# A transformer block in fp32: a new order for its beginning and its end, and a modulation moved between two heads

## The chip, the core and the metric

The kernel runs on one core of a Trainium2 chip. The metric is the device time of one execution in microseconds (us). A core has TensorE (PE, matrix products, with weight loads beside them), VectorE (DVE), ScalarE (ACT), GpSimd (POOL) and SyncE (SP, which here only issues DMA transfers). Each engine works through its own list of instructions in order and waits on semaphores for the others. PE writes into PSUM, eight banks of 128 partitions x 512 fp32 values; DVE and ACT read from there.

## What is computed

One block with adaptive layer norm for two sequences (B = 2) of 1024 rows of 256 values: 16 heads of 128, and a gated feed-forward layer of 704 hidden values with quantised weights.

```python
mod = (silu(c) @ wmod).reshape(B, 6, 1, -1)        # c is 2 x 256
sa, ca, ga, sb, cb, gb = the six parts of mod
ga = (2 * (ga >= 0) - 1) * maximum(abs(ga), 0.25)  # gb likewise
h = layernorm(x) * (1 + ca) + sa
x = x + ga * attention(h)       # rotary q, k; causal softmax; biases on q, k, v, out
h = layernorm(x) * (1 + cb) + sb
x = x + gb * (W_down(silu(W_gate h) * (W_up h)))   # W = (wq - 128) * scale per row
```

## The kernel before

All products are fp32, and PE runs each as two passes, so the profile counts two matmuls for one in the code. A layer norm is split: `ln_stats` and `ln_scale` (DVE) and `ln_sqrt` (ACT) make normalised rows `xn`, `ln_turn` transposes a block of four row tiles on PE, 128 x 128 at a time, and writes `hT` with scale and shift, one half by DVE and (with `split`) one by ACT. Later layer norms inside the loop over heads go another way, by DVE transposes and DMAs (`ln_move`, `ln_send`, `ln_shift`). `modulation(which, ...)` makes shift and scale columns as products of wmod with SiLU(c); `gates` makes the two gate rows and spreads them over the partitions through DRAM.

The order of work is written out by hand (`tc.manual_schedule`), so program order is the order on each engine. It has three stages.

- The beginning (lines 646 to 693): constants, loads, the first layer norm, q, k and v of the first head in two blocks of 512 rows. On SP the loads are issued in the order x tiles 0 and 1, half of the first wmod block, x tiles 2 and 3, the other half, wq, wk, half of the rotary tables, wv, x tiles 4 to 7, the other half of the tables, wga, the second wmod block, the weights of later heads. ACT issues c (as a column over 128 partitions) and the biases. `warm_up` products of ones keep PE occupied while the loads are under way: three at the start and one after each of the four groups of the first modulation.
- The loop over 32 heads (lines 695 to 735), index n, with eight steps i each: scores of row block i, the masked maximum on DVE, the exponential on ACT, DVE transposes of the probabilities in blocks of 32, 32 DMAs per head issued by SP to complete the transposition (pT), products with the values, the output projection; and beside them the projections of the next head. `extras` places further work; the modulation of the second layer norm and its `shift_scale` stand there at n = 0, i = 6.
- The end (lines 737 to 770): the last hidden chunks (`hidden`, six per block of 512 rows, the sixth of 64 + 64 rows), the last layer norm blocks, the down products (`down`) and the stores.

PSUM is divided into pools: ps_a (two banks), ps_o and ps_y (one each), ps_sc (two pairs of banks, for scores of up to 1024 columns). A tile taken from a pool waits until the previous holder of its bank has been read. `bank` deals out y, o, a, a in turn at the end. In SBUF, `rot` has two buffers (tag r1), `xnp` four; outputs of the first block of the first sequence use `rot`, the others `xnp`.

In `down`, the sixth chunk has only 64 rows; these rows lie in the upper half of the partitions for odd row tiles and in the lower half for even ones, so that two such passes run at the same time. They come after the five full chunks, for two row tiles at a time (first block of the first sequence, last block of the second) or for all four.

Of the kernel before, what the change touches and what calls it, by code (L numbers as in the profile page):

```python
# [37 lines left out]
def adaln_block(ctx: ExitStack, tc: tile.TileContext, a, cos_d, sin_d, out):  # L38
# [21 lines left out]
    wmod = fpool.tile([P, 2, KC, 2 * D], F32, tag="f", name="wmod")  # L60
# [5 lines left out]
    nc.scalar.dma_start(sc, a["L0_c"])  # L66
    for n in range(KC):
        load_x(0, 2 * n, 2, nc.sync)
        half = slice(n * D, (n + 1) * D)
        nc.sync.dma_start(wmod[:, 0, :, half], a["L0_wmod"][0, :, :, half])  # L70
    nc.scalar.dma_start(cols, a["biases"])

# [11 lines left out]
    for n in range(3):  # L84
        warm_up(4)
# [26 lines left out]
    def modulation(which, pool, tag):  # L112

        pm = pool.tile([P, 512], F32, tag=tag, name=f"pm{which}")
        for n in range(2):
            for f in range(KC):
                at = (n * KC + f) * B
                for k in range(KC):
                    nc.tensor.matmul(
                        pm[:, at : at + B],  # L120
                        wmod[:, which // 2, k, n * D + f * P : n * D + (f + 1) * P],
                        sc[:, :, k],
                        start=(k == 0),
                        stop=(k == KC - 1),
                    )
                if not which:
                    warm_up(1)
        pms[which] = pm
# [3 lines left out]
    def shift_scale(which):  # L132
        pm = pms[which]
        for n in range(2):
            nc.vector.tensor_scalar(
                modT[:, which + n].rearrange("p f b -> p (f b)"),
                pm[:, n * KC * B : (n + 1) * KC * B],
                float(n),
                None,
                ALU.add,  # L140
            )
# [3 lines left out]

    def gates():

        pg = ps_y.tile([P, 512], F32, tag="y", name="pg")
        for k in range(KC):
            nc.tensor.matmul(pg[:B], sc[:, :, k], wga[:, k, :], start=(k == 0), stop=(k == KC - 1))  # L150
# [55 lines left out]
    def ln_turn(b, name, blk, which, dest, split=False):  # L206
        for f in range(KC):
            pt = ps_a.tile([P, 512], F32, tag="a", name=f"ptx_{name}{b}_{blk}_{f}")
            for j in range(4):
                nc.tensor.transpose(  # L210
                    pt[:, ts(j, P)], xns[b, name, 4 * blk + j][:, ts(f, P)], ident
                )
            shift, scale = (modT[:, which + n, f, b : b + 1] for n in range(2))
            if split and f:
                nc.scalar.activation(dest[:, f, :], pt, AF.Identity, bias=shift, scale=scale)
            else:
                nc.vector.tensor_scalar(dest[:, f, :], pt, scale, shift, ALU.mult, ALU.add)  # L217
# [135 lines left out]
    def project_v(b, g, t, pool=ps_a, tag="a"):  # L353
# [3 lines left out]
        pv = pool.tile([P, 512], F32, tag=tag, name=f"pv_{b}{g}{t}")  # L357
# [167 lines left out]
    def hidden(b, blk, c, late=True):  # L525
        if c == 0:
# [33 lines left out]
    def down(b, blk, *js):  # L560

        pds = {}
        for j in js:
            pds[j] = bank(f"pd_{b}{blk}{j}")
            for c in range(NF - 1):
                nc.tensor.matmul(  # L566
                    pds[j][:, :D],
                    gTs[b, blk][:, c, ts(j, P)],
                    wdT[b][:, c, :],
                    start=(c == 0),  # L570
                    stop=False,
                )
        for j in js:
            half = ts(j % 2, HID - FULL)
            nc.tensor.matmul(  # L575
                pds[j][:, :D],
                gTs[b, blk][half, NF - 1, ts(j, P)],
                wdT[b][half, NF - 1, :],
                start=False,
                stop=True,  # L580
            )
        for j in js:
            t = blk * 4 + j
            if (b, blk) == (0, 0):
# [254 lines left out]
```

## Time and profile before

| what | value |
|---|---|
| median of three runs | 1082.43 us (1082.18 to 1083.43) |
| profiled execution: own time | 1084.72 us |
| profiled execution: span, first to last instruction | 1082.9 us |
| PE busy | 1071.2 us, 99% of the span |
| DVE, ACT, POOL busy | 655.9, 508.0, 397.2 us |
| granted PE clock over the span | 1.000 |
| first 11 us: PE busy | 8.88 us |
| 11 to 25 us: PE busy | 13.56 of 14 us |
| 48 to 968 us: PE busy | 916.98 of 920 us |

A row of a timeline gives the start, the length, the engine, the line of the kernel, the operation and its operands (out<-in), how often it came in a row and, in brackets, how long the engine had stood idle before it and what released it. The releaser is inferred; where the named one cannot be meant, another event of the same moment is. Busy time of pipelined matmuls overlaps, so four passes of 0.59 each take 1.72 in all (0.43 apart), and the profile's "4 in 1.88" is that plus the drain of the last. The chain of work that ended last is read backwards from the end of the span; 95% of it is PE.

### The profile page before, as it was taken

How to read it: one execution, taken by the hardware profiler on the slowest of the kernel's cores; microseconds unless marked ns; L12 is line 12 of the kernel's file. 1: busy time of each engine (PE TensorE's matmuls, PEld its weight loads, DVE VectorE, ACT ScalarE, POOL GpSimd, SP SyncE). 2: the span in 40 equal slices, each digit the busy share in tenths (PEclk: the TensorE clock that was granted, in tenths of full speed). 3: DMA queues.
4: the chain of work that ended last, by engine and by line, in shares of the span. 5: the costliest groups of instructions: out<-in, count | busy, mean ns of one | idle time of the engine just before them, and what ended most of it. 6: DMA issues, size and time to landing. Idle time of an engine off the chain costs nothing.

```text
span 1082.9 us, 12350 instructions
## 1 busy us (share of the span) xinstructions
PE 1071.2 (99%) x3524; PEld 638.8 (59%) x3524; DVE 655.9 (61%) x1422; ACT 508.0 (47%) x956; POOL 397.2 (37%) x364
## 2 busy tenths in 40 slices
PE   8999999999999999999999999999999999999998
PEld 5556555666656655556565666665655566555656
DVE  5566566667767776556666665666667766454321
ACT  4644454455445544445445444454455445652110
POOL 4635353534344343654343433333333334100000
PEclk9999999999999999999999999999999999999999
DMA  6355655657564556565564645454656556422001
GB/s 211 91 137 126 168 141 127 165 126 182 117 147 99 141 120 153 117 142 131 114 146 107 146 109 144 97 142 93 149 117 141 131 125 139 97 66 51 20 20 39
DMA packets 66615, 130.97 MB, mean 121 GB/s; under 512 B 18898, under 2 KB 22226, under 8 KB 66548
## 3 DMA queue, kind: packets, MB, share of 16 engines
q1 hardware_dynamic: 64772, 125.91, 49.3%
q10 hardware_dynamic: 1728, 4.16, 1.1%
q8 instruction: 28, 0.46, 0.2%
q14 instruction: 39, 0.32, 0.1%
q0 software_dynamic: 48, 0.13, 0.1%
HBM read 25.26 MB, written 2.10 MB: 25 GB/s over the span
## 4 chain that ended last, share of the span: by engine, by line
PE 95%; DMA 1%; SPq 1%; DVE 1%; ACT 1%; issue 0%; POOL 0%; DVEq 0%; ACTq 0%
PE po L483 23%; PE ps L422 22%; PE pv L361 10%; PE pq L379 10%; PE pk L379 10%; PE py L509 10%; PE pgu L538 6%; PE pd L566 3%; DMA pT<-t 1%; SPq L468 1%; DMA wmod<-in_wmod 0%; PE pd L575 0%; ACT L557 0%; PE ptx_b L210 0%; DVE t L456 0%
## 5 line engine op out<-in xcount | busy, mean ns | idle before, releaser
L442 ACT ACTIVATE p<-ps,nmax 128x128 f32<-128x128 f32 (+7 forms) x256 | 189.8, 741 | 413.1 <-DVE nmax L425 413.0
L422 PE MATMUL ps<-kT,qT 128*128 128x512 f32 (+3 forms) x768 | 289.5, 486 | 0.7 <-DMA pT<-t 0.7
L425 DVE CUSTOM_DVE_ANT_0 ps<-ps,mask 128x128 f32<-128x128 f32 (+7 forms) x256 | 195.5, 764 | 129.0 <-PE ps L422 128.5
L483 PE MATMUL po<-pT,v 128*128 128x512 f32 (+3 forms) x768 | 264.0, 487 | 2.5 <-issue 1.5
L512 DVE SCALAR_TENSOR_TENSOR x<-py,rden,x 128x256 f32<-128x256 f32 x256 | 122.8, 482 | 185.3 <-PE py L509 177.8
L483 PEld LDWEIGHTS po<-pT,v 128*128 128x128 f32 x768 | 145.1, 190 | 134.1 <-issue 109.8
L456 DVE STREAM_TRANSPOSE t<-p 128x128 f32<-128x128 f32 (+7 forms) x256 | 198.1, 774 | 1.1 <-DMA x<-in_x 0.6
L422 PEld LDWEIGHTS ps<-kT,qT 128*128 128x128 f32 x768 | 145.7, 190 | 77.5 <-issue 63.1
L392 POOL TENSOR_TENSOR r_k<-r_k,sin_t 128x512 f32<-128x512 f32 x64 | 81.2, 1270 | 224.4 <-ACT r_k L391 224.4
L509 PE MATMUL py<-wo,o 128*128 128x256 f32 x512 | 151.3, 379 | 0.0
L398 POOL TENSOR_TENSOR kT<-kT,r_k 128x512 f32<-128x512 f32 x64 | 81.3, 1270 | 140.7 <-DVE rden L506 117.6
L392 POOL TENSOR_TENSOR r_q<-r_q,sin_t 128x512 f32<-128x512 f32 x64 | 81.7, 1277 | 137.5 <-ACT r_q L391 122.6
L509 PEld LDWEIGHTS py<-wo,o 128*128 128x128 f32 x512 | 92.6, 190 | 65.1 <-issue 53.1
L361 PE MATMUL pv<-wv,hT 128*128 128x256 f32 x512 | 121.0, 379 | 1.1 <-DVE qT L395 1.1
L379 PE MATMUL pq<-hT,wq 128*128 128x512 f32 x256 | 120.6, 593 | 0.5 <-DVE hT L217 0.5
L379 PE MATMUL pk<-hT,wk 128*128 128x512 f32 x256 | 120.3, 592 | 0.0
L361 PEld LDWEIGHTS pv<-wv,hT 128*128 128x128 f32 x512 | 94.9, 190 | 19.9 <-DVE qT L395 1.2
L391 ACT ACTIVATE r_q<-pq,cols 64x512 f32<-64x512 f32 x128 | 87.4, 683 | 23.4 <-PE pq L379 21.8
L398 POOL TENSOR_TENSOR qT<-qT,r_q 128x512 f32<-128x512 f32 x64 | 83.6, 1306 | 31.8 <-DVE qT L395 28.9
L391 ACT ACTIVATE r_k<-pk,cols 64x512 f32<-64x512 f32 x128 | 87.4, 683 | 6.0 <-PE pk L379 0.4
L379 PEld LDWEIGHTS pk<-hT,wk 128*128 128x128 f32 x256 | 48.6, 190 | 54.6 <-issue 44.7
L379 PEld LDWEIGHTS pq<-hT,wq 128*128 128x128 f32 x256 | 46.1, 190 | 33.8 <-issue 31.2
(89 smaller groups left out, 688.0 us busy)
## 6 DMA issues: line engine op xcount, KB each, us to landing
pT<-t SPq DMA_DIRECT2D x512, 128.0 KB, 2.4
pT<-t SPq DMA_DIRECT2D x512, 64.0 KB, 2.0
wq<-in_Wq SPq DMA_DIRECT2D x16, 256.0 KB, 3.0
wk<-in_Wk SPq DMA_DIRECT2D x16, 256.0 KB, 3.9
wv<-in_Wv SPq DMA_DIRECT2D x16, 256.0 KB, 4.1
wo<-in_Wo SPq DMA_DIRECT2D x16, 256.0 KB, 2.9
out<-yo SPq DMA_DIRECT2D x16, 128.0 KB, 1.8
x<-in_x SPq DMA_DIRECT2D x4, 256.0 KB, 5.3
```

Of the source, the lines that this page charges most:

```text
L361: nc.tensor.matmul(pv[:, ts(j, HG * DH)], hT[b, n][:, k, ts(r, P)], weights[b, g]["v"][:, k, :], start=(k == 0), stop=(k == KC - 1),)
L379: nc.tensor.matmul(pq, weights[b, g][s][:, k, ts(h, DH)], hT[b, n][:, k, :], start=(k == 0), stop=(k == KC - 1),)
L391: nc.scalar.activation(r1[to], pq[of], AF.Identity, bias=cols[of, c : c + 1])
L392: nc.gpsimd.tensor_tensor(r1, r1, sin_t[:, sl], ALU.mult)
L398: nc.gpsimd.tensor_tensor(dst[:, sl], dst[:, sl], r1, ALU.add)
L422: nc.tensor.matmul(ps[:, c:e], qT[:, ts(i, P)], kT[:, c:e], start=True, stop=True)
L425: nc.vector.tensor_tensor_reduce(ps[:, :L], ps[:, :L], mask[:, NT - 1 - i :, :].rearrange("p t k -> p (t k)"), -SCALE, FLT_MAX, ALU.add, A ...
L442: nc.scalar.activation(p[:, :L], ps[:, :L], AF.Exp, bias=nmax, scale=-1.0, accum_out=dens[u][:, i : i + 1])
L456: nc.vector.transpose(t32[blk][:, :, j, : i + 1, :].rearrange("p c k b -> p k c b"), p[:, : (i + 1) * P].rearrange("p (k c a) -> p k c a", ...
L483: nc.tensor.matmul(po[:, off * P :], vs[b, g][:, k, ts(h, DH)], pT[:, off:, :, k, :], start=(k == 0), stop=(k == last),)
L509: nc.tensor.matmul(py[:, :D], outs[u][:, ts(t, P)], weights[b, g]["o"][:, h, :], start=True, stop=True)
L512: nc.vector.scalar_tensor_tensor(x[b][:, t, :], py[:, :D], rdens[u][:, t : t + 1], x[b][:, t, :], ALU.mult, ALU.add)
```

## The change

- Loads: c comes as four rows of 128 and is transposed on PE before its SiLU. x tile 0 is loaded alone, tile 1 from ACT's queue, tiles 2 and 3 before wmod. wmod's layout is by output half, each half a separate contiguous load. wga is loaded ahead of wq. x tiles 4 and 5 come before wv.
- Warm-up: one product at the start and two behind the transpose of c; none in the modulation, whose moving operand is the same two columns repeated to 128.
- The gates' product is done in two parts, one behind each of the first two turns. The second turn (`wide`) takes a pair of ps_sc banks and stands behind one pair of value products instead of two; the second pair follows it, on ps_sc. In head 0 the other value products take ps_o.
- The second modulation moves from n = 0, i = 6 (ps_a) to n = 1, i = 0 (ps_y); head 0's first product with the values from step 1 of head 1 to step 2, behind that step's value projection.
- The end: the first of the late turns takes ps_sc, the second moves behind the first hidden chunk of the next block. `down` does four row tiles at once. In the last hidden block the sixth chunk comes first; the last `down` starts with the 64-row products and stores each tile when it is done, the last one in two parts of 128 columns.

```diff
-    wmod = fpool.tile([P, 2, KC, 2 * D], F32, tag="f", name="wmod")
+    wmod = fpool.tile([P, 2, 2, KC, D], F32, tag="f", name="wmod")
     wga = fpool.tile([P, KC, 2 * D], F32, tag="f", name="wga")
...
-    nc.scalar.dma_start(sc, a["L0_c"])
-    for n in range(KC):
-        load_x(0, 2 * n, 2, nc.sync)
-        half = slice(n * D, (n + 1) * D)
-        nc.sync.dma_start(wmod[:, 0, :, half], a["L0_wmod"][0, :, :, half])
+    def load_wmod(block, n, eng):
+        eng.dma_start(wmod[:, block, n], a["L0_wmod"][block, n])
+    row_c = rot.tile([P, QB], F32, tag="r1", name="row_c")[: B * KC, :P]
+    nc.scalar.dma_start(row_c, a["L0_c"])
+    load_x(0, 0, 1, nc.sync)
+    load_x(0, 1, 1, nc.scalar)
+    load_x(0, 2, 2, nc.sync)
     nc.scalar.dma_start(cols, a["biases"])
+    for n in range(2):
+        load_wmod(0, n, nc.sync)
...
-    for n in range(3):
-        warm_up(4)
+    warm_up(4)
...
         pm = pool.tile([P, 512], F32, tag=tag, name=f"pm{which}")
+        wide = pm.rearrange("p (n f r b) -> p n f r b", n=2, f=KC, b=B)
         for n in range(2):
             for f in range(KC):
-                at = (n * KC + f) * B
                 for k in range(KC):
                     nc.tensor.matmul(
-                        pm[:, at : at + B],
-                        wmod[:, which // 2, k, n * D + f * P : n * D + (f + 1) * P],
-                        sc[:, :, k],
+                        wide[:, n, f],
+                        wmod[:, which // 2, n, k, ts(f, P)],
+                        sc[:, :, k].unsqueeze(1).to_broadcast([P, P // B, B]),
                         start=(k == 0),
...
                     )
-                if not which:
-                    warm_up(1)
-        pms[which] = pm
+        pms[which] = wide
...
         for n in range(2):
-            nc.vector.tensor_scalar(
-                modT[:, which + n].rearrange("p f b -> p (f b)"),
-                pm[:, n * KC * B : (n + 1) * KC * B],
-                float(n),
-                None,
-                ALU.add,
-            )
+            nc.vector.tensor_scalar(modT[:, which + n], pm[:, n, :, 0, :], float(n), None, ALU.add)
...
+    pgs = []
+    def gates_product(k):
+        if k == 0:
+            pgs.append(ps_y.tile([P, 512], F32, tag="y", name="pg"))
+        nc.tensor.matmul(pgs[0][:B], sc[:, :, k], wga[:, k, :], start=(k == 0), stop=(k == KC - 1))
     def gates():
...
-        pg = ps_y.tile([P, 512], F32, tag="y", name="pg")
-        for k in range(KC):
-            nc.tensor.matmul(pg[:B], sc[:, :, k], wga[:, k, :], start=(k == 0), stop=(k == KC - 1))
+        pg = pgs.pop()
         sgn = ppool.tile([P, S], F32, tag="p", name="sgn")[:B, :QB]
...
-    def ln_turn(b, name, blk, which, dest, split=False):
+    def ln_turn(b, name, blk, which, dest, split=False, wide=False):
+        tag = f"ptx_{name}{b}_{blk}"
+        if wide:
+            both = ps_sc.tile([P, S], F32, tag="sc", name=tag)
+            pts = [both[:, ts(f, QB)] for f in range(KC)]
+        else:
+            pts = [ps_a.tile([P, 512], F32, tag="a", name=f"{tag}_{f}") for f in range(KC)]
         for f in range(KC):
-            pt = ps_a.tile([P, 512], F32, tag="a", name=f"ptx_{name}{b}_{blk}_{f}")
             for j in range(4):
                 nc.tensor.transpose(
-                    pt[:, ts(j, P)], xns[b, name, 4 * blk + j][:, ts(f, P)], ident
+                    pts[f][:, ts(j, P)], xns[b, name, 4 * blk + j][:, ts(f, P)], ident
                 )
+        for f in range(KC):
             shift, scale = (modT[:, which + n, f, b : b + 1] for n in range(2))
             if split and f:
-                nc.scalar.activation(dest[:, f, :], pt, AF.Identity, bias=shift, scale=scale)
+                nc.scalar.activation(dest[:, f, :], pts[f], AF.Identity, bias=shift, scale=scale)
             else:
-                nc.vector.tensor_scalar(dest[:, f, :], pt, scale, shift, ALU.mult, ALU.add)
+                nc.vector.tensor_scalar(dest[:, f, :], pts[f], scale, shift, ALU.mult, ALU.add)
...
-    def project_v(b, g, t, pool=ps_a, tag="a"):
+    def project_v(b, g, t, pool=ps_a, tag="a", width=512):
...
             vs[b, g] = vpool.tile([P, NT, HG * DH], F32, tag="v", name=f"v_{b}{g}")
-        pv = pool.tile([P, 512], F32, tag=tag, name=f"pv_{b}{g}{t}")
+        pv = pool.tile([P, width], F32, tag=tag, name=f"pv_{b}{g}{t}")[:, :512]
         for j in range(2):
...
-    def hidden(b, blk, c, late=True):
-        if c == 0:
+    def hidden(b, blk, c, late=True, first=None):
+        if c == 0 if first is None else first:
             gTs[b, blk] = fpool.tile([P, NF, QB], F32, tag="f", name=f"gT_{b}{blk}")
...
-    def down(b, blk, *js):
-        pds = {}
-        for j in js:
-            pds[j] = bank(f"pd_{b}{blk}{j}")
+    def down(b, blk):
+        end = (b, blk) == (1, 1)
+        pds = [bank(f"pd_{b}{blk}{j}") for j in range(4)]
+        parts = [(j, pds[j], slice(0, D)) for j in range(4)]
+        if end:
+            rest = ps_sc.tile([P, S], F32, tag="sc", name=f"pd_{b}{blk}r")
+            parts[3:] = [(3, pds[3], slice(0, P)), (3, rest, slice(P, D))]
+        def halves():
+            for j, pd, cols in parts:
+                half = ts(j % 2, HID - FULL)
+                nc.tensor.matmul(
+                    pd[:, cols],
+                    gTs[b, blk][half, NF - 1, ts(j, P)],
+                    wdT[b][half, NF - 1, cols],
+                    start=end,
+                    stop=not end,
+                )
+        def chunks(j, pd, cols):
             for c in range(NF - 1):
                 nc.tensor.matmul(
-                    pds[j][:, :D],
+                    pd[:, cols],
                     gTs[b, blk][:, c, ts(j, P)],
-                    wdT[b][:, c, :],
-                    start=(c == 0),
-                    stop=False,
+                    wdT[b][:, c, cols],
+                    start=(c == 0 and not end),
+                    stop=(c == NF - 2 and end),
                 )
-        for j in js:
-            half = ts(j % 2, HID - FULL)
-            nc.tensor.matmul(
-                pds[j][:, :D],
-                gTs[b, blk][half, NF - 1, ts(j, P)],
-                wdT[b][half, NF - 1, :],
-                start=False,
-                stop=True,
-            )
-        for j in js:
+        def store(j, pd, cols):
             t = blk * 4 + j
-            if (b, blk) == (0, 0):
-                yo = rot.tile([P, D], F32, tag="r1", name=f"yo_{b}{t}")
-            else:
-                yo = xnp.tile([P, D], F32, tag="xn", name=f"yo_{b}{t}")
-            nc.vector.tensor_tensor(yo, pds[j][:, :D], x[b][:, t, :], ALU.add)
-            nc.sync.dma_start(out[b, ts(t, P), :], yo)
+            if cols.start == 0:
+                if (b, blk) == (0, 0):
+                    yos[t] = rot.tile([P, D], F32, tag="r1", name=f"yo_{b}{t}")
+                else:
+                    yos[t] = xnp.tile([P, D], F32, tag="xn", name=f"yo_{b}{t}")
+            yo = yos[t]
+            nc.vector.tensor_tensor(yo[:, cols], pd[:, cols], x[b][:, t, cols], ALU.add)
+            nc.sync.dma_start(out[b, ts(t, P), cols], yo[:, cols])
+        yos = {}
+        if end:
+            halves()
+            for part in parts:
+                chunks(*part)
+                store(*part)
+            return
+        for part in parts:
+            chunks(*part)
+        halves()
+        for part in parts:
+            store(*part)
...
             fold_out(*units[n][:2])
-        if n == 0 and i == 6:
-            modulation(2, ps_a, "a")
+        if n == 1 and i == 0:
+            modulation(2, ps_y, "y")
             shift_scale(2)
...
     with tc.manual_schedule():
-        nc.scalar.activation(
-            sc.rearrange("p b k -> p (b k)"), sc.rearrange("p b k -> p (b k)"), AF.Silu
-        )
+        pc = ps_a.tile([P, 512], F32, tag="a", name="pc")
+        nc.tensor.transpose(pc[:, : B * KC], row_c, ident[: B * KC, : B * KC])
+        warm_up(4)
+        warm_up(2)
+        nc.scalar.activation(sc.rearrange("p b k -> p (b k)"), pc[:, : B * KC], AF.Silu)
         nc.scalar.activation(warm, eps_t, AF.Sqrt)
         weights[0, 0] = {}
+        nc.sync.dma_start(wga, a["w_gates"])
         load_w(0, 0, "q")
...
             nc.sync.dma_start(t[:, :QB], t_d[:, :QB])
+        load_x(0, 4, 2, nc.sync)
         load_w(0, 0, "v")
-        for t in (4, 6):
-            load_x(0, t, 2, nc.sync)
+        load_x(0, 6, 2, nc.sync)
         for t, t_d in ((cos_t, cos_d), (sin_t, sin_d)):
             nc.sync.dma_start(t[:, QB:], t_d[:, QB:])
-        nc.sync.dma_start(wga, a["w_gates"])
-        nc.sync.dma_start(wmod[:, 1], a["L0_wmod"][1])
+        for n in range(2):
+            load_wmod(1, n, nc.sync)
         load_proj(*units[2][:2])
...
             ln_sqrt(0, "a", t, t + 2)
-            if t:
-                ln_scale(0, "a", 0, (0, 1))
-        modulation(0, ps_y, "y")
+        modulation(0, ps_o, "o")
+        ln_scale(0, "a", 0, (0, 1))
         ln_scale(0, "a", 0, (2, 3))
...
         ln_turn(0, "a", 0, 0, new_hT(0, 0), split=True)
+        gates_product(0)
         for t in range(4, NT):
...
             project_qk(units[0], s, 0)
-        for t in (0, 2):
-            project_v(0, 0, t, *((ps_o, "o"), (ps_y, "y"))[t // 2])
+        project_v(0, 0, 0, ps_o, "o")
         ln_scale(0, "a", 1)
         release()
-        ln_turn(0, "a", 1, 0, new_hT(0, 1), split=True)
+        ln_turn(0, "a", 1, 0, new_hT(0, 1), split=True, wide=True)
+        gates_product(1)
+        project_v(0, 0, 2, ps_sc, "sc", S)
         gates()
...
                     values(u, 0, 0, 4)
-                if n == 1 and i == 1:
-                    values(prev, 0, 0, 4)
                 if i in (0, 2):
                     if h == 0:
-                        project_v(b, g, 4 + i)
+                        project_v(b, g, 4 + i, *((ps_a, "a") if n else (ps_o, "o")))
                     elif more:
                         project_v(nb, ng, i)
+                if n == 1 and i == 2:
+                    values(prev, 0, 0, 4)
                 if not nxt and i < NF:
...
         hidden(0, 1, 5)
-        ln_turn(1, "b", 0, 2, new_h2(1, 0))
+        ln_turn(1, "b", 0, 2, new_h2(1, 0), wide=True)
         for t in range(4, NT):
...
         ln_sqrt(1, "b", 4, NT)
-        down(0, 0, 0, 1)
         ln_scale(1, "b", 1)
-        down(0, 0, 2, 3)
-        ln_turn(1, "b", 1, 2, new_h2(1, 1))
+        down(0, 0)
         for c in range(NF):
             hidden(1, 0, c)
+            if c == 0:
+                ln_turn(1, "b", 1, 2, new_h2(1, 1))
             if c == 3:
-                down(0, 1, 0, 1, 2, 3)
-        for c in range(NF):
-            hidden(1, 1, c)
-            if c == 3:
-                down(1, 0, 0, 1, 2, 3)
-        down(1, 1, 0, 1)
-        down(1, 1, 2, 3)
+                down(0, 1)
+        order = (NF - 1, *range(NF - 1))
+        for c in order:
+            hidden(1, 1, c, first=(c == order[0]))
+            if c == order[3]:
+                down(1, 0)
+        down(1, 1)
...
     args["L0_attn_bo"] = given("in_bo", v["L0_attn_bo"].reshape(1, D))
-    args["L0_c"] = given("in_c", np.moveaxis(v["L0_c"].reshape(B, KC, P), 2, 0))
+    args["L0_c"] = given("in_c", v["L0_c"].reshape(B * KC, P))
     wmod = v["L0_wmod"].reshape(D, 2, 3, D)
-    args["L0_wmod"] = given(
-        "in_wmod", by_partition(np.moveaxis(wmod[:, :, :2], 1, 0).reshape(2, D, 2 * D), 1)
-    )
+    args["L0_wmod"] = given("in_wmod", by_partition(np.moveaxis(wmod[:, :, :2], 0, 2), 2))
     args["w_gates"] = given("in_w_gates", by_partition(wmod[:, :, 2].reshape(D, 2 * D)))
...
```

## The prediction

> **What bounds the kernel now.** I read the page's busy shares, then the list of what TensorE (PE) waited for, then timelines of the beginning and the end, because the change touches only these.
>
> ```profile
> PE 1071.2 (99%) x3524; PEld 638.8 (59%) x3524; DVE 655.9 (61%) x1422; ACT 508.0 (47%) x956; POOL 397.2 (37%) x364
> ...
> PE pv L361 <- DVE qT L395: 1.1, 1, 1.1
> ...
> PE ptx_b L210 <- DVE x L512: 0.8, 1, 0.8
> PE ps L422 <- DMA pT<-t: 0.7, 1, 0.7
> PE ptx_b L210 <- DVE yo L588: 0.5, 1, 0.5
> PE pq L379 <- DVE hT L217: 0.5, 1, 0.5
> ```
>
> PE is busy nearly throughout, so time can be won only where PE stands still, where it does work that is dropped, and behind its last matmul. The waits above are single ones, all near the two ends. The timelines place them (start, length, count, idle before):
>
> ```profile
> 1.13 4.29 PE L82 MATMUL warm_ps<-ones 128*128 128x512 f32 x6 [1.13 <-POOL ones L76]
> ...
> 7.52 0.61 PE L119 MATMUL pm<-sc,wmod 128*128 128x2 f32 x4
> ...
> 8.96 1.45 PE L210 MATMUL ptx_a<-ident,xn_a 128*128 128x128 f32 x8
> 10.88 1.98 PE L379 MATMUL pq<-hT,wq 128*128 128x512 f32 x4 [0.47 <-DVE hT L217]
> ...
> 18.83 1.88 PE L150 MATMUL pg<-wga,sc 128*2 128x512 f32 x4
> ...
> 24.18 0.38 PE L422 MATMUL ps<-kT,qT 128*128 128x128 f32 x2
> 25.62 1.99 PE L361 MATMUL pv<-wv,hT 128*128 128x256 f32 x8 [1.05 <-DVE qT L395]
> ...
> 41.85 1.84 PE L119 MATMUL pm<-sc,wmod 128*128 128x2 f32 x16
> ...
> 48.20 0.70 PE L422 MATMUL ps<-kT,qT 128*128 128x256 f32 x2 [0.73 <-DMA pT<-t]
> ...
> 998.75 1.09 PE L210 MATMUL ptx_b<-ident,xn_b 128*128 128x128 f32 x8 [0.76 <-DVE x L512]
> ...
> 1078.49 0.70 PE L575 MATMUL pd<-wdT,gT 64*128 64x256 f32 x4
> ```
>
> The reader sees the first projection at 10.88, the first score at 24.18, and stops of 1.05, 0.73, 0.76 and 0.51 us. The release at 48.20 is mislabelled: a score does not read pT, and ACT's accumulator read of the last exponential ended at 48.14; that exponential frees the score bank. All terms below come from this execution (span 1082.9, own time 1084.72; the median of the three timed runs is 1082.43).
>
> **A. Up to the first projection (10.88 now).** The modulation must wait for wmod. The loads land about 0.65 to 0.75 us per 256 KB: by the starts of their readers x tiles 0 and 1 at 4.30, the first wmod half at 5.85, x tiles 2 and 3 at 6.75, the second half at 7.52. Now the x tiles come first: tile 1 is moved to ACT's queue (one issue more there, some 0.4 us, ahead of a table load that has slack), tiles 2 and 3 land where the first half did (5.85), the halves at 6.75 and 7.5. Statistics of tiles 2 and 3 take 1.1 (to 6.95), the four normalisations with two reciprocals 1.75 (to 8.7). The modulation's 16 passes stand at 0.11 each (16 in 1.84 in head 0); the second eight run 7.65 to 8.55, and the four warm-ups between them (0.33 each) are gone. A free size of 128 instead of 2 should not change that: the transposes, 128 wide, also stand at 0.11. Transposes end at 9.3. The first half of the gates' product, two 512-wide passes of 0.43, runs in the gap in which hT is written (0.9 wide) to 10.15; hT's DVE half is done at about 9.95. wga is moved ahead of wq on SP and past eight other loads. It is 512 KB, so wq, which landed at about 8.15 (issue 3.15 plus 5.0), lands near 9.5, wk 10.3: in time. First projection at 10.15: **-0.73**. Bounds: -1.4 (loads with fewer small packets land 0.7 earlier) and +0.6 (wq 1.3 later still).
>
> SiLU of c now waits for a 4-row load, a PE transpose and ACT. The load is bounded by the 4 KB gate row (1.24 to its reader) and the old column load (3.7); I take 2, being nearest to the first in descriptors, so sc is ready before 4.5, well ahead of wmod at 6.75. At 3.7 it is still ready at about 5.
>
> **B. First projection to first score (13.46 now, 10.88 to 24.34 in the chain).** The PE work is: two projections 3.44, value products 3.45, transposes 0.87, gates 0.86 instead of 1.72, two projections 3.44, in all 12.1. But x tiles 4 and 5 land 256 KB later (12.4 instead of 11.75), 6 and 7 512 KB later (13.7). Four statistics on DVE then end at 14.85, ACT's root at 15.15, the normalised rows come at 15.8, 16.15, 16.5, 16.85. PE, having only one pair of value products (1.73) before the turn, is there at 15.3 and waits about 1.1. The second gates' half (0.86) and the second value pair (1.73) then cover the eviction: behind the root ACT does r_q, r_k, the value copy and hT by 19.35; DVE does qT, kT, hT by 19.55; PE ends its cover at 19.9. Queued behind the late root on ACT are r_q and r_k, hence POOL's kT: ready at 21.8, needed at 23.4. The gates' four DVE operations (2.7) come behind hT, 19.55 to 22.3, before the first maximum; their store and four loads on SP find an empty queue, as now. Of the other loads moved on SP, x tiles 4 and 5 pass wv (needed at 13.6, landing 13.1) and wmod's second block becomes two issues that nobody waits for before head two. First score at 23.4, **-0.2** relative to A. Bounds: -1.3 (rows in time) and +0.8 (tiles 6 and 7 another microsecond late).
>
> **C. The stop of 1.05 at 25.62** is a value product that waits for a bank of ps_a; it takes ps_o now, which ACT's copy freed around 18.6. With PE's refill **-1.1**. Next in line is ps_o's second use (i = 2), whose copy ends near 27.4 against 28.2. Bounds -1.2 and 0 (if ps_o is held).
>
> **D. The second modulation** moves from 41.85 into the stop at 47.47 to 48.20. Its 1.84 are longer than the stop: **-0.73**. The exponential that ends the stop moves with PE, because DVE waited 1.59 for PE before that head's last maximum. Its DVE work, two ops of 0.15, sits in front of a maximum whose score PE computes afterwards anyway. The first value product moves one step back, behind 0.65 + 1.73 of other work. That matters: its pT needs 16 SP issues of about 0.64, from 37.34, landing by some 50.4, just ahead of 50.66. With PE 2.9 earlier and the issues 2 earlier, it would be late at its old place by 0.9 and has 1.4 of slack at the new one. Bounds -0.8 and +0.5.
>
> **E. Before the end.** The first late transposes go to ps_sc, free at 997.24: **-0.76**; the down products behind them find their banks evicted (997.9 to 999.1). The second ones go behind a 3.43 hidden chunk: **-0.51**. Four outputs at once share two rot buffers, so outputs 3 and 4 wait for stores of 1.8, and DVE stands 2 us; the two ps_a banks come free at about 1011.4 and 1011.8, the transposes ask at 1012.0. One group of eight 64-row passes (1.06) for two of four (0.63 + 0.68): **-0.25**. Bounds for the three: -1.6 and -0.9 (the banks 0.6 late).
>
> **F. The end.** Now: chunks 4.32 + 4.51, 64-row 0.63 + 0.68. After: ten 64-row passes, 1.06 plus two 128-wide of 0.11, say 1.28; three full products of 2.16; two halves of ten passes at 0.11, 2.23; sum 9.99 for 10.14: **-0.15**. The 64-row passes also hide the last SiLU and product (0.6 + 0.69). Behind PE two serial DVE additions (0.76) become one of half width, about 0.28: **-0.48**. The last store is half as large; its landing I leave at 1.78. Bounds -0.9 and +0.9 (128-wide passes bounded by their weight load's 0.19: 20 passes more by 0.08, less the rest).
>
> Sum: -0.73 - 0.2 - 1.1 - 0.73 - 1.52 - 0.63 = **-4.9**. From 1084.72 that is 1079.8; from the median, 1077.5. The heads between (48 to 968, PE 917 of 920) keep their order, so shifts pass through. About 0.2%, 2.2 us, is what can be told from no change.
>
> **A rule against the change.** In the profile the clock shows itself: the first warm-up passes, 512 wide, average 0.715, the later projections 0.43. The change cuts warm-ups and leaves PE idle from about 5 to 6.75. The Trainium skill, "TensorE: Matmul & The Clock Gate", section "Why this matters for your kernels", asks for 4 us of continuous work and no gaps above about 3 us; by it the thinner warm-up could leave PE at half rate through a few microseconds of work more, about 1.7 given back, and the sum would be -3.2 instead of -4.9. The gap is under its limit, and no row here shows a relapse.
>
> **Rivals.**
> 1. *Everything lands earlier*: no stall at the second turn, and A by its lower bound. -4.9 - 1.1 - 0.5 = -6.5: 1075.9. For it: the 2 KB load that is spread over 128 rows (16 bytes each) leaves the busy beginning. Against: the other bytes are the same, with wga ahead.
> 2. *The front is eaten by loads*: A at 0, B at +0.6. -3.4: 1079.0. For it: wga's 512 KB in front of all that is needed at once.
> 3. *The front's gain is given back at the first value product*, because pT's SP issues do not move: C and D lost, -3.1: 1079.3. Against: the issues start on DVE's transposes, which PE drives.
> 4. *Slower: the clock.* PE falls to half rate in the idle gap at 5 to 6.75. Each us of PE work from 6.75 on then costs another; the cost outweighs -4.9 if PE needs more than 4.9 us of its work (9.8 of time) at half rate, until about 16.5, and at +6 the kernel takes 1083.5. Against: the old warm-up was through within 5.4 us, so such a state should last about 4: cost 2, 1079.5.
>
> **How the numbers follow.** Forecast 0.50, first rival 0.14, second 0.14, third 0.10, fourth 0.10 (slower 0.07, no change 0.03), anything else 0.02. Faster by over 0.2% holds the first four (0.88) but for their tails toward small gains (0.05): 0.83; within 0.2%: that tail, 0.03 and half of the rest, 0.09; slower: 0.08. Forecast's own range: 1076.3 to 1079.2. Leaving a tenth at each end: 1075.3 to 1080.9.
>
> **What would show it.** First projection at 10.15; a wait of the second transposes on xn near 16; no idle before pv at i = 0; modulation without idle before the next score; no idle at the late transposes; one 128x128 addition at the end. Wrong if early 512-wide passes stand at 0.85, or wq's landing sets the first projection, or PE waits for pT in head two.

## The result: 1082.37 to 1078.30 us

The changed kernel takes 1078.30 us in the median of six runs (1076.70 to 1079.23), the kernel before 1082.37 (1081.95 to 1083.63). The ratio is 0.9957, with a 95% interval of 0.9945 to 0.9970: faster by 4.1 us, between 3.2 and 6.0. A second timing, told below, gave 0.9953 (0.9940 to 0.9967). The forecast was 1077.5, that is -4.9.

The page and the list of PE's waits of the changed kernel (last columns of the waits: total, times, longest):

```profile
span 1075.1 us, 12365 instructions
...
PE 1068.8 (99%) x3529; PEld 639.0 (59%) x3529; DVE 656.8 (61%) x1423; ACT 507.2 (47%) x956; POOL 397.1 (37%) x364
...
PE pm L125 <- DMA wmod<-in_wmod: 1.3, 1, 1.3
PE warm_ps L88 <- POOL ones L82: 1.1, 1, 1.1
PE po L492 <- DMA pT<-t: 0.5, 1, 0.5
PE pgu L547 <- ACT sg L566: 0.3, 1, 0.3
```

The five single stops that carried the prediction (pv, ps, two of ptx_b, pq) are gone from the list; grown is PE's wait for wmod (1.3, and 0.5 in a second profile; 0.4 in the kernel before). PE's timeline, at the places shown of before:

```profile
1.13 2.08 PE L88 MATMUL warm_ps<-ones 128*128 128x512 f32 x2 [1.13 <-POOL ones L82]
3.13 0.26 PE L682 MATMUL pc<-ident,row_c 4*128 4x4 f32 x1
...
6.83 2.02 PE L125 MATMUL pm<-sc,wmod 128*128 128x128 f32 x16 [1.33 <-DMA wmod<-in_wmod]
8.69 1.49 PE L218 MATMUL ptx_a<-ident,xn_a 128*128 128x128 f32 x8
10.11 1.02 PE L149 MATMUL pg<-wga,sc 128*2 128x512 f32 x2
11.06 1.98 PE L388 MATMUL pq<-hT,wq 128*128 128x512 f32 x4
...
16.32 1.56 PE L218 MATMUL ptx_a<-ident,xn_a 128*128 128x128 f32 x8
...
24.03 0.38 PE L431 MATMUL ps<-kT,qT 128*128 128x128 f32 x2
24.25 1.89 PE L370 MATMUL pv<-wv,hT 128*128 128x256 f32 x8
...
44.14 1.95 PE L125 MATMUL pm<-sc,wmod 128*128 128x128 f32 x16
45.93 0.59 PE L431 MATMUL ps<-kT,qT 128*128 128x256 f32 x2
...
992.77 1.04 PE L218 MATMUL ptx_b<-ident,xn_b 128*128 128x128 f32 x8
...
1071.02 1.28 PE L592 MATMUL pd_11r<-wdT,gT 128*128 128x128 f32 x10
```

The first projection starts no earlier than before (11.06 for 10.88), but the first score is followed at once by its value product, the modulation leads into the next score without idle time, and the late transposes come 6 us earlier (3.3 in the second profiles; the heads in between vary).

The two profiled spans differ by 7.8 us (1082.9 and 1075.1), the timed medians by 4.1. So both kernels were profiled once more. The table gives the sections between marked starts on PE's timeline, in us, with the forecast of the letter that belongs to each. The end of the last hidden product is the start of its last pass plus one pass of 0.43.

| section | before, two profiles | after, two profiles | change | forecast |
|---|---|---|---|---|
| to the first projection | 10.88, 10.56 | 11.06, 11.00 | +0.3 | A -0.73 |
| to the first score | 13.30, 13.41 | 12.97, 13.08 | -0.33 | B -0.2 |
| to the value product of step 0 | 1.44, 1.44 | 0.22, 0.22 | -1.22 | C -1.1 |
| to the score of step 1, head 1 | 22.58, 22.58 | 21.68, 21.68 | -0.90 | D -0.73 |
| to the late transposes | 950.55, 948.31 | 946.84, 947.02 | -1.3 to -3.7 | E, first part, -0.76 |
| to the end of the last hidden product | 70.19, 70.19 | 69.39, 69.39 | -0.80 | E, rest, -0.76 |
| to the end of the span | 14.01, 14.01 | 12.93, 12.94 | -1.07 | F -0.63 |

The 32 heads are the only section that does not repeat within 0.4 us. Without their own stops (-0.76 of it taken for E, which an experiment below shows) the sum is +0.3 - 0.33 - 1.22 - 0.90 - 0.76 - 0.80 - 1.07 = -4.8. The first two rows cancel: the first score stands at 24.03 and 24.08 after, at 24.18 and 23.97 before, so all of the gain comes from behind it.

### The profile page after: what moved, and what is told of

The parts are those of the page before. It is cut to its first block, busy times and chain, and to the rows that moved or that the text cites. A ratio compares the mean times of both kernels' runs of the same rounds, so it can differ in the third digit from the quotient of the medians.

```text
span 1075.1 us, 12365 instructions
## 1 busy us (share of the span) xinstructions
PE 1068.8 (99%) x3529; PEld 639.0 (59%) x3529; DVE 656.8 (61%) x1423; ACT 507.2 (47%) x956; POOL 397.1 (37%) x364
## 4 chain that ended last, share of the span: by engine, by line
PE 98%; DMA 1%; ACT 0%; issue 0%; DVE 0%; SPq 0%; DVEq 0%; ACTq 0%
PE po L492 23%; PE ps L431 23%; PE pv L370 10%; PE pq L388 10%; PE pk L388 10%; PE py L518 10%; PE pgu L547 7%; PE pd L592 3%; DMA wmod<-in_wmod 0%; PE pd L582 0%; PE pm L125 0%; PE ptx_a L218 0%; ACT L566 0%; DMA pT<-t 0%; PE pg L149 0%; PE ptx_b L218 0%
```

## The experiments

All but the kernel before are the changed kernel with the edit shown. A run that puts one step back was executed once. The times of these runs (1077.6 to 1079.7 us) lie within or near the changed kernel's own range and decide nothing; stops and sections on the timeline are compared.

**Both kernels' own spread.** The kernel before, unedited.

> The kernel before, profiled once more. The two spans differ by 7.8 us, the medians of the timed runs by only 4.1. Theory M (the difference is waits of the value products for pT between 48 and 968 us, which differ from one execution to the next): the stops before value products in that stretch, 2.5 us in the first profile of before, come out at other places or with another sum (0.5 to 3), and the beginning and the end repeat within 0.1. Rival (the changed kernel removes them by its shift): they stand at the same places with 2.3 to 2.7 in all.

Its span was 1080.5, 2.4 less than in the first profile. Waits of PE in this profile:

```profile
PE po L483 <- DMA pT<-t: 0.8, 1, 0.8
PE ptx_b L210 <- DVE x L512: 0.8, 1, 0.8
PE ps L422 <- DMA pT<-t: 0.7, 1, 0.7
PE ptx_b L210 <- DVE yo L588: 0.5, 1, 0.5
```

Stops before value products stood at 74, 180, 444, 592, 739 and 857 us in the first profile (2.5 in all, idle time on PE's timeline), and at 180 and 855 in this one (1.07). In the changed kernel they were 0.7 and, in its second profile, 0.8; in the runs below that put one step back, 0.5 to 2.0. Theory M holds: these waits come and go between executions of one program. The single stops near the two ends repeat to 0.01. The beginning does not repeat within 0.1, as was expected: the first projection starts at 10.56 instead of 10.88.

**C alone.** The value products of head 0 go back to ps_a.

```diff
-project_v(b, g, 4 + i, *((ps_a, "a") if n else (ps_o, "o")))
+project_v(b, g, 4 + i)
```

> The changed kernel with one edit: the value products of head 0 take ps_a again instead of ps_o. Prediction's step C: PE idles about 1.05 us before the value product of step 0 (at about 24.2), because both banks of ps_a hold projections that DVE has not yet read, and everything behind is later by 1.1. Rival (ACT and DVE are now so far ahead, through the earlier gates, that the banks are free): idle below 0.4.

```profile
23.94 0.38 PE L431 MATMUL ps<-kT,qT 128*128 128x128 f32 x2
25.50 1.99 PE L370 MATMUL pv<-wv,hT 128*128 128x256 f32 x8 [1.18 <-DVE qT L404]
```

The stop is back, at 1.18, and the section grows from 0.22 to 1.56; the next one, to the score of step 1 of head 1, takes 21.78 instead of 21.68. C stands: the bank made the wait, and the rest of the change had not shortened it.

**D, its modulation.** Back to step 6 of head 0.

```diff
-        if n == 1 and i == 0:
-            modulation(2, ps_y, "y")
+        if n == 0 and i == 6:
+            modulation(2, ps_a, "a")
```

> The changed kernel with one edit: the second modulation goes back to step 6 of head 0 (ps_a). Theory (the modulation fills a stop that an exponential on ACT sets): the stop comes back, PE idles 0.6 to 0.8 us before the score of step 1 in head 1, that score starts at about 46.6 instead of 45.93, and ACT's accumulator read of the exponential before it ends within 0.1 of it. Rival (the stop was set by a pT transfer, as the profile's label says): pT's issues start as early as in the changed kernel, so no stop above 0.2 and the score stays at 45.9.

The timeline of all engines around the stop:

```profile
45.10 1.11 ACT L451 ACTIVATE p<-ps,nmax 128x1024 f32<-128x1024 f32 x1 [2.09 <-DVE nmax L434]
...
46.12 0.19 ACT L451 ACTIVATION_READ_ACCUMULATOR p<-ps,nmax 128x1 f32 x1
46.36 0.30 PEld L431 LDWEIGHTS ps<-kT,qT 128*128 128x128 f32 x2 [1.13 <-ACT p L451]
46.36 0.70 PE L431 MATMUL ps<-kT,qT 128*128 128x256 f32 x2 [0.73 <-DMA pT<-t]
```

PE idles 0.73 again, to the hundredth as before, and starts 0.05 after ACT's accumulator read ends (46.31). The weight load's row names ACT, the matmul's row a pT transfer; the product with pT stands elsewhere now, behind another step, and the stop is the same. So it is ACT's exponential, as read in the prediction. The section to this score is 22.48 instead of 21.68.

**D, the value product.** Back to step 1 of head 1.

```diff
+                if n == 1 and i == 1:
+                    values(prev, 0, 0, 4)
                 if i in (0, 2):
...
-                if n == 1 and i == 2:
-                    values(prev, 0, 0, 4)
```

> The changed kernel with one edit: head 0's first product with the values goes back to step 1 of head 1, where it stood before. Prediction's step D: its pT is late there by 0.9 us, so PE waits about 0.9 for a pT transfer behind the projection at 48.1, and the score of step 2 starts that much later. Rival: pT's issues move with PE as a whole, and there is no wait above 0.2.

```profile
46.16 1.88 PE L388 MATMUL pq<-hT,wq 128*128 128x512 f32 x4
48.94 2.40 PE L492 MATMUL po<-pT,v 128*128 128x512 f32 x8 [0.89 <-DMA pT<-t]
```

A wait of 0.89, where 0.9 was forecast. The step by which the product moved is what keeps this part of C's and D's gain. The third rival (given back at the first value product) is thus half right, and the change avoids it: the loss is 0.89 and not C and D whole, and pT's issues do move, their first from 37.34 in the kernel before to 35.87 in the changed kernel.

**E, its first part.** The first late turn takes ps_a again (`wide=True` left out).

> The changed kernel with one edit: the first of the late turns takes ps_a again instead of ps_sc. Prediction's step E, first part: PE idles about 0.76 us before the late transposes, for DVE's additions that read the output projections in these banks. Rival (the earlier parts have given DVE so much room that the banks are read): idle below 0.2.

```profile
PE po L492 <- DMA pT<-t: 1.3, 2, 0.7
...
PE ptx_b L218 <- DVE x L521: 0.8, 1, 0.8
```

The stop before the late transposes is back (0.76 on the timeline).

**F.** The last `down` has the form of the others.

```diff
-        end = (b, blk) == (1, 1)
+        end = False
...
-        order = (NF - 1, *range(NF - 1))
+        order = range(NF)
```

> The changed kernel with the end of the last down undone: chunks in the order 0 to 5, the 64-row products last, whole 256-wide tiles, all four additions behind them. Prediction's step F: four DVE additions in a row instead of one of half width behind PE, and the 64-row products on the path. By the rows of the down before it, which has that form (four additions in 1.42), the time from PE's last matmul to the end of the span grows from 2.8 to about 4.1 (1.42 for 0.29), PE's part shrinks by 0.1 to 0.3; in sum +0.9 to +1.3. Rival (the stores set the end: they are issued early in either form): below +0.4.

DVE's timeline at the end, this kernel first and the changed kernel second:

```profile
1073.31 1.41 DVE L608 TENSOR_TENSOR yo<-pd,x 128x256 f32<-128x256 f32 x4 [7.76 <-PE pd L582]
```

```profile
1070.11 0.42 DVE L608 TENSOR_TENSOR yo<-pd,x 128x256 f32<-128x256 f32 x1 [1.74 <-PE pd L592]
1071.22 0.29 DVE L608 TENSOR_TENSOR yo<-pd,x 128x128 f32<-128x128 f32 x1 [0.69 <-PE pd L592]
1072.34 0.29 DVE L608 TENSOR_TENSOR yo<-pd_11r,x 128x128 f32<-128x128 f32 x1 [0.82 <-PE pd_11r L592]
```

From PE's last matmul to the end of the span 4.19 instead of 2.80; PE's own part 9.86 instead of 10.14, since one group of eight 64-row passes is cheaper than ten passes and the split. Together +1.1. But the section before it, from the late transposes to the end of the last hidden product, is 0.19 shorter here (69.20 for 69.39): so much the sixth chunk in first place costs. In all +0.9, at the lower edge of what was expected.

**The clock.** Without the two warm-up products behind the transpose of c.

```diff
-        warm_up(4)
-        warm_up(2)
```

> The changed kernel without the two warm-up products behind the transpose of c; PE then does 1.9 us of products, up to 3.2 us, and idles until wmod lands near 6.9. Theory cold (the clock needs continuous work): the first modulation passes stand at 0.2 us and more instead of 0.11, and the first projection starts 1.5 to 3 us later than 11.06. Rival (the clock, once started or by itself, is full by then): the passes stand at 0.11 and the first projection at 10.8 to 11.1.

```profile
3.13 0.26 PE L682 MATMUL pc<-ident,row_c 4*128 4x4 f32 x1
6.71 3.75 PE L125 MATMUL pm<-sc,wmod 128*128 128x128 f32 x16 [3.31 <-DMA wmod<-in_wmod]
10.26 1.24 PE L218 MATMUL ptx_a<-ident,xn_a 128*128 128x128 f32 x8
11.43 1.02 PE L149 MATMUL pg<-wga,sc 128*2 128x512 f32 x2
12.38 1.98 PE L388 MATMUL pq<-hT,wq 128*128 128x512 f32 x4
```

The sixteen passes take 3.75 instead of 2.02 (starts 0.213 apart instead of 0.11), and by the starts of the transposes' passes the half rate lasts until 10.7, 4.0 us after work resumed. The first projection is 1.3 later, less than the 1.5 to 3 expected; 0.5 of it comes back at the second turn, which then no longer waits, so the first score is 0.8 later (24.82). The profile's granted clock reads 1.00 in this stretch too; only the spacing of the passes shows the half rate. This is the fourth rival's mechanism, switched on. It agrees with the section "Why this matters for your kernels" of the Trainium skill's "TensorE: Matmul & The Clock Gate" (continuous work of about 4 us to reach the full clock): 2.1 us of warm-up and a gap of 3.3 were too little here. Warm-up until 5.5 and a gap of 1.3 were enough in the changed kernel's first profile, but not in its second:

```profile
3.33 2.93 PE L88 MATMUL warm_ps<-ones 128*128 128x512 f32 x4
6.71 2.53 PE L125 MATMUL pm<-sc,wmod 128*128 128x128 f32 x16 [0.45 <-DMA wmod<-in_wmod]
```

Here PE worked almost without a break from 1.13 to 6.26, which is 5.1 us, and the modulation's first passes still stand 0.21 apart, until 7.7; from then on it is 0.11. So 4 us of continuous work did not suffice in this execution, and when the full rate comes differs from one execution to the next. It cost no time: the first projection starts at 11.00, since the transposes then had no wait for their rows (1.03 for 1.49).

**A, the queue of x tile 1.**

```diff
-    load_x(0, 1, 1, nc.scalar)
+    load_x(0, 1, 1, nc.sync)
```

> The changed kernel with one edit: x tile 1 is loaded from SP's queue instead of ACT's. In the changed kernel tile 0's statistics start at 3.12 us and tile 1's at 5.99. Theory Q (tile 1 is late because it runs on ACT's queue): its statistics start before 4.5, tiles 2 and 3 follow when they land, the normalised rows are done about 0.5 earlier (8.8 instead of 9.3) and the first projection starts at 10.5 instead of 11.06. Rival B (tile 1 is late because the bytes of the other loads are in the way, whatever the queue): it starts at about 5.9 again and the first projection stays within 0.15 of 11.06.

DVE's first statistics in the changed kernel (tile 0, then tile 1); with tile 1 on SP (tile 1, then tile 2); and tile 1 in the next experiment, where it is on SP too:

```profile
3.12 0.43 DVE L188 BATCH_NORM_STATS2 st_a<-x 128x6 f32<-128x256 f32 x1 [3.12 <-DMA x<-in_x]
...
5.99 0.43 DVE L188 BATCH_NORM_STATS2 st_a<-x 128x6 f32<-128x256 f32 x1 [2.23 <-DMA x<-in_x]
```

```profile
4.65 0.43 DVE L188 BATCH_NORM_STATS2 st_a<-x 128x6 f32<-128x256 f32 x1 [0.87 <-DMA x<-in_x]
...
6.31 0.43 DVE L188 BATCH_NORM_STATS2 st_a<-x 128x6 f32<-128x256 f32 x1 [1.01 <-DMA x<-in_x]
```

```profile
5.49 0.43 DVE L188 BATCH_NORM_STATS2 st_a<-x 128x6 f32<-128x256 f32 x1 [1.25 <-DMA x<-in_x]
```

Tile 1 comes at 4.65 instead of 5.99 here. In the eight profiles with tile 1 on ACT's queue its statistics start at 5.81 to 5.99, in the four with it on SP at 4.28, 4.65, 5.46 and 5.49. So the queue makes it late (theory Q), by 0.3 to 1.7 us; how much of that is the load of c ahead of it on ACT's queue was not tried. But the first projection starts at 10.85, not at 10.5: now wmod holds it (PE's first modulation pass at 7.08, not 6.83), and PE works without a stop from there: 16 passes, eight transposes, two passes of the gates' product, 3.8 in all. The gain of 0.2 is small but repeats: 10.73 to 10.85 in the four profiles, 10.88 to 11.06 in seven with ACT's queue (the one without warm-ups left out).

**Loads in another order.** Tile 1 on SP, and further:

```diff
-        nc.sync.dma_start(wga, a["w_gates"])
+        nc.sync.dma_start(wga[:, 0], a["w_gates"][:, 0])
         load_w(0, 0, "q")
         load_w(0, 0, "k")
+        load_x(0, 4, 2, nc.sync)
+        load_x(0, 6, 2, nc.sync)
+        load_w(0, 0, "v")
         for t, t_d in ((cos_t, cos_d), (sin_t, sin_d)):
             nc.sync.dma_start(t[:, :QB], t_d[:, :QB])
-        load_x(0, 4, 2, nc.sync)
-        load_w(0, 0, "v")
-        load_x(0, 6, 2, nc.sync)
+        nc.sync.dma_start(wga[:, 1], a["w_gates"][:, 1])
```

> The changed kernel with two edits of the loads: x tile 1 on SP's queue, and wga loaded in two halves of 256 KB (the one that the first part of the gates' product needs where wga stood, the other behind all loads of the first head), with x tiles 4 to 7 ahead of wv and the rotary tables. Theory (the second turn waits for x tiles 4 to 7, which wga and the tables hold up): their statistics end near 13 instead of 15.0, the eight transposes of the second turn take 1.0 instead of 1.6 us, and the first score starts 0.6 to 1.0 earlier than 24.03; in time -0.7 against the changed kernel, 1077.6, ratio to before about 0.9955. Rival (the row's lateness is DVE's and ACT's own work, or the loads behind become late in turn: wv or the tables): first score within 0.3 of 23.9 and no gain.

```profile
10.76 1.98 PE L388 MATMUL pq<-hT,wq 128*128 128x512 f32 x4
...
16.02 1.04 PE L218 MATMUL ptx_a<-ident,xn_a 128*128 128x128 f32 x8
...
23.20 0.38 PE L431 MATMUL ps<-kT,qT 128*128 128x128 f32 x2
```

The second turn takes 1.04 instead of 1.56, its rows are ready before PE asks, and the first score comes 0.82 earlier than in the changed kernel. That is B's stall, with its cause: x tiles 4 to 7 landing behind wga, wv and the tables (tile 1 on SP alone leaves the first score at 23.90; which of the loads ahead of them counts most was not tried). In time the ratio to before is 0.9948 (0.9935 to 0.9961).

**The two side by side on one chip.**

> The changed kernel once more, timed in five rounds beside the kernel before and beside the next two. The sum by the profile's terms in the beginning and the end is -4.9 of span; the stops of the value products in between, 0.8 to 2.8 us in the profiles so far in both kernels, are noise to it. Expected ratio 0.9955 with an interval of about 0.001 either way.

> The kernel with the two edits of the loads (first score at 23.2 instead of 24.03), timed on the same chip as the changed kernel. Theory: the 0.8 won before the first score passes through to the end, median 0.5 to 1.1 below the changed kernel. Rival: it is lost in the heads, or too small beside the value products' stops: within 0.4.

Changed kernel 1077.41 (1077.09 to 1079.13), new order of loads 1077.18 (1076.38 to 1080.00), before 1083.54; ratios 0.9953 (0.9940 to 0.9967) and 0.9947 (0.9934 to 0.9960). The profiles show the first score at 24.08 in the changed kernel and at 23.17 in the new order. In time the new order's median is lower by 0.2, within the rival's 0.4, and the intervals overlap: a gain is not shown by the times, only by the timeline, and the value products' own stops are larger than it.

**The stops in the heads.** On top of the new order, the second block's products with the values stand together at step 6.

```diff
-                if i in (5, 6) and prev:
-                    values(prev, 1, 4 * (i - 5), 4 * (i - 4))
+                if i == 6 and prev:
+                    values(prev, 1, 0, 8)
```

> As both_loads2, and in each head the second block's products with the values stand together at step 6 instead of being split between steps 5 and 6, so that their pT has about 1.9 us more to land. Theory (the stops of 0.1 to 1.0 in the heads are pT transfers that land just too late behind 32 SP issues of 0.6): stops before value products between 60 and 930 us fall from 1.2 (0.5 to 2.0) to below 0.3, time -0.5 to -1.5. Rival (the score of step 6 then comes 3.4 us earlier, before ACT has freed its bank): stops before scores in all heads, some 0.3 us in each of 31, time +5 or more.

```profile
PE py L518 <- DVE x L521: 2.3, 4, 0.7
PE pm L125 <- DMA wmod<-in_wmod: 1.4, 1, 1.4
...
```

No value product waits any more, so the stops were indeed pT landing just too late. But 2.3 us of others take their place: in heads whose DVE also does layer norm work (at 352, 382, 823 and 853 us), the output projection waits for DVE to free its only bank. The time is 1080.58, ratio 0.9970 (0.9958 to 0.9981), 3.4 above its base; the profiled spans differ by 1.9 (1076.5 and 1074.6), so the stops explain a part of it only, and the rest stays open. The rival had the right sign, another place (scores were expected to wait) and a smaller size than it said.

## Why the prediction was right, point by point

The total was near: -4.9 forecast, -4.8 by the sections, and -4.1 and -6.1 in the medians of the two timings. C, D, E and F came, for the reasons given. The front did not: A and B were to give -0.93 by the first score and gave nothing. That the sum still fits is luck, because the parts behind gave 0.8 more than forecast.

- **A failed**: -0.73 forecast, +0.3 measured. The step that failed first is "tile 1 is moved to ACT's queue", which gave that queue no delay. Tiles 2 and 3 did land as forecast (5.76 by the trace, for 5.85), but tile 1 took 4.7 us from its issue (1.30) to its reader, tile 0 on SP 2.4, and DVE takes the tiles in order. The statistics ended at 7.6 instead of 6.95 and the rows at 9.3 instead of 8.7. The experiment shows that this is only 0.2 of the error. The rest is in "Transposes end at 9.3" and in the gates' product that was to fit "in the gap in which hT is written" to 10.15: wmod's first pass came 0.1 (0.3 with tile 1 on SP) later than its place in the old order said, PE's row of work from there is 3.8 and not 3.4, and the gates' pair does not fit into the gap, it ends 0.46 after DVE has written hT (10.85 against 10.39 with tile 1 on SP). The base moves too: 10.88 and 10.56 in the two profiles of the kernel before.
- **B**: -0.2 forecast, -0.33 measured, and near by two errors that cancel. The second turn's wait, forecast at about 1.1, came out at 0.5: the rows were there at 15.7 to 17.0 against 15.8 to 16.85 forecast, but PE asked at 16.3 instead of 15.3, because A was late. Against that, PE's own work in this section, summed to 12.1, takes 12.44 where nothing waits (the new order of loads): the rows in which PE changes between transposes, gates and projections are 0.1 longer each. By these rows B would have lost most of what A lost in any case; that is argued, no run shows it.
- **The second rival** was right that loads eat the front's gain, and 0.6 too pessimistic in size: with half of wga, wv and the tables behind x tiles 4 to 7 the first score comes 0.8 earlier.
- **C**: -1.1 forecast, -1.22 measured, shown alone. ps_o's second use did not wait.
- **D**: -0.73 forecast, -0.90 measured in its section. The modulation put back alone makes this section 0.80 longer, and the value products put back on ps_a alone make it 0.10 longer, so 0.1 of the 0.90 belongs to C. The move of the value product is shown alone as well.
- **E**: -1.52 forecast; 0.76 for the first part shown alone, 0.80 for the rest by the sections only. In these 0.80 the 0.19 is already paid that the sixth chunk in first place costs, so the rest of E is nearer to 0.99. The stand of DVE behind the two rot buffers came (yo pairs at 1003.10 and 1005.41), and PE did not notice.
- **F**: -0.63 forecast, -1.07 measured in its section, -0.9 with the 0.19 taken off. PE's part (-0.12) and DVE's addition (0.29 for 0.76) were as forecast. Mis-sized is the term that said "its landing I leave at 1.78": SP's wait for the last store, of 64 KB, ended 1.56 after its issue. Two things were not in the sum: the last store no longer queues behind the issue of the one before it (0.1), and no other wait stands behind it in SP's closing list, where three of 0.06 each stood before (0.2).
- **The clock** (fourth rival): in the first profile the gap came (1.33) and the modulation's passes stand 0.11 apart. In the second, full rate came only at 7.7, in the midst of the modulation, and cost nothing, as wmod had come 0.1 earlier and the rows set the pace of the transposes. No row shows a fall during the gap; that the late rise was harmless is luck of this order, and the experiment without warm-ups shows what it costs when it comes later still.
- **The heads between** were said to pass shifts through. They do, on average, but add 0.7 to 2.5 us of their own stops for pT in the four profiles, different in each execution. The prediction's bounds left these out, and they are as large as half of the forecast.

## What to carry to other kernels

Where one engine is busy 99% of the span, list its single stops and ask of each which bank or transfer ends it: a stop of 1.2 us vanished because a product took another PSUM bank, one of 0.73 because movable work was put into it. A part won at the start is safe only if what follows is not paced by something else; here the first value product had to move by one step, or 0.89 of what the parts ahead of it won would have been given back to a queue of DMA issues. A moved load has to be checked for the whole list of loads behind it, and two profiled spans of one program should be compared before the difference of two programs is explained. The same holds for the clock: one profile showed the thin warm-up to be enough, the next did not.

## What was not expected of the hardware

A load on another issuing queue can be later, and hold up the first queue too. In the changed kernel, SP's issues stand like this (start, length):

```profile
3.05 0.43 SPq L315 DMA_DIRECT2D wq<-in_Wq  x1
3.53 0.65 SPq L315 DMA_DIRECT2D wk<-in_Wk  x1
5.98 0.33 SPq L692 DMA_DIRECT2D cos_t<-rotary_cos  x1
```

Between wk and cos_t SP issued nothing for 1.8 us. The next transfer uses the semaphore of x tile 1, in the instruction's operands, so it waited until that tile had landed (5.97; its reader starts at 5.99). With tile 1 on SP the same issue waits for the semaphore of the biases, which are on ACT's queue too, and stands at 4.84:

```profile
4.00 0.52 SPq L315 DMA_DIRECT2D wk<-in_Wk  x1
4.84 0.33 SPq L692 DMA_DIRECT2D cos_t<-rotary_cos  x1
```

The Trainium skill, "DMA: Bandwidth & Descriptors", section "Issuing engines are not separate DMA queues", says that transfers of all issuers interleave on the same engines and that a second issuer saves only issue time. The saved issue time is there: SP issues tiles 2 and 3 at 1.17 instead of 1.63, and they land at 5.76 instead of 6.29. But it is not the only effect: tile 1 itself came later than from SP, by 1.3 us in these two profiles and by 0.3 to 1.7 over all, although it was issued about as early (1.30, and 1.17 on SP).
